# Local-attention transformer block, two calls per kernel: where the layer norm's root is computed, and where a unit's closing work stands among the attention steps

## The chip, the cores and the metric

The kernel runs on one core of a Trainium2 chip, as a single launch. The metric is device time in microseconds (us), taken over several runs, of which the median counts. In the profile the engines are called PE (TensorE, matmul and transpose), PEld (TensorE loading its stationary operand), DVE (VectorE), ACT (ScalarE), POOL (GpSimd) and SP (SyncE, which here only starts DMAs). All data is float32.

## The reference, cut to what matters

The program is four transformer layers in one kernel, each as "half feed-forward, attention, half feed-forward". The change touches only the feed-forward of layer 3, which is itself a small transformer of depth 2 with local attention. It is called twice, with different inputs and the same weights, and the attention of layer 3 (`l3_attn`) stands between the two calls:

```python
x = x + 0.5 * _L3_ffn_ref(_layernorm(x), ...)   # first call
x = x + _L3_attn_ref(_layernorm(x), ...)
x = x + 0.5 * _L3_ffn_ref(_layernorm(x), ...)   # second call, the end of the program
```

`x` has 4 sequences of 512 rows and 128 features. `_L3_ffn_ref` runs this layer twice (8 heads of 64 features, windows of 64 rows, 341 hidden features):

```python
def _layer(x, wqkv, qs, ksc, wo, lg, lb, w1, b1, w2, b2):
    h = shift_token(x)                       # second half of the features comes from the row before
    q, k, v = split(h @ wqkv)                # to 8 heads of 64
    q, k = l2norm(q) * qs, l2norm(k) * ksc   # each head's row divided by its norm
    q, k = rotary_xpos(q, k)
    o = local_attention(q, k, v)             # own window of 64 and the one before; mask, softmax
    x = x + o @ wo
    h = shift_token(x)
    h = (h - mu) / sqrt(var + 1e-05) * lg + lb
    a, g = split(h @ w1 + b1)
    return x + (a * gelu(g)) @ w2 + b2
```

## The kernel before

**Units and steps.** `l3_ffn(w3, tag, first, rb)` is emitted once per call (`first` is true for the first). Its work is 8 *units*: depth 0 for the sequences 0 to 3, then depth 1 for the same sequences. A unit has `TB` = 4 *steps*, one for each 128 rows, so there are 32 steps. The feature-major activations of a sequence lie in `yT`; `x` and `y` are row-major.

**One step** is cut in six parts. The names in brackets are the tiles by which the profile's rows can be followed.

- `project`: the products with the weights of q and k [`p_qk`] and of v [`pv`]; ScalarE squares q and k [`sq`]; VectorE multiplies `p_qk` with the rotary tables in three instructions [`t<-p_qk,w`] and sums the squares to 16 norms a row [`rn`]; `inverse_root` makes the inverse norms of them [scratch `ir`]; GpSimd adds the two rotary parts [`t<-t,t`, L1850] and scales k by its inverse norms [`t<-t,rn`, L1851]; v is copied, and a DMA moves half of it to `vb`.
- `to_features`: eight transposes of q and k [`pt_qk`], copied to `qT` (ScalarE) and `kT` (VectorE).
- `weights`: the products of q and k [`ps`], VectorE's mask addition [`s`], the negative row maximum [`nm`] and its product with q's inverse norms [`nm<-nm,rn`].
- `exponentials`: eight ScalarE instructions, one for each head, with a row sum each [`sm`]; the reciprocal on VectorE, and the product `s<-s,sm` on GpSimd (L1917).
- `turn_weights`: eight transposes [`pt`], copied to `PT`.
- `with_values`: the products with v [`po`], copied to `oT`.

**The closing work of a unit** follows its fourth step: `summed` (product with `wo` [`pz`], added to `yT`), `shifted` (the shifted copy `h`), `centred` (the mean by a product with a constant [`pm`], subtracted: `h<-h,pm`), `squared` (ScalarE, `sq<-h`), `variance` (a product with the same constant [`pvar`], copied to `rs`, and then the root by `inverse_root`), `spread` (VectorE makes diagonal blocks of the root [`dg`]), `normed` (their product [`pb`] scales `h`), three times `hidden` (the two products [`pag`], gelu [`ge`], their product [`hh`]), `close_unit` (product with `w2` [`pz2`], added to `yT`) and, after depth 1, `leave` (transposed back [`pt_z`], added to `x`; in the first call `leave_normed` then starts the next layer norm for `l3_attn`, in the second the rows are stored). `attended` is `summed` and `shifted`, `mean` is `centred` and `squared`. All these take a slice `at` of the unit's 512 rows.

**The order of the work.** A loop over `n` runs from -2 to 37 and emits the six parts in this order, each with a lag, so that several steps are in flight:

```python
for place, (part, lag) in enumerate((
    (project, 0), (to_features, 2), (exponentials, 4), (weights, 3), (turn_weights, 5), (with_values, 6)
)):
    for f, u in later.pop((n, place), ()):
        f(u)
```

A unit's closing work is put among these by a table `parts`: each entry is a function, a number added to `4 * u` to give `n`, and the place ahead of which it is emitted. `squared` has the place `MIDST`, inside `exponentials` after its fifth instruction (`i == 4`). `norm_unit` (the first layer norm of a sequence of depth 0, if the work before the call has not done it) and `open_unit` (the unit's shifted copy `hT`) stand ahead of a unit's first step, at 2 and 1 loop turns.

TensorE and ScalarE execute the products and activations of this layer in the order in which they are emitted. VectorE's and GpSimd's instructions are ordered by the scheduler when the program is built, by what they need; the order of that built program is what the prediction calls the built order.

The last unit (`last` = 7) is not in the table. Its closing work follows the loop as a list `rest`; in the first call it is spread as a *chain* over the start of `l3_attn`, in the second each function is emitted for the first 256 rows and then for the second 256 rows, with `leave` of the unit before behind `attended`.

A chain is a queue of functions with gaps. `tick()`, called after each of the six places (and at such places in `l3_attn`), advances a clock, and a chain's next function is emitted once its gap has passed. `leave_normed(b, chain(b), gap)` puts three functions on one: the row statistics after 1 tick, the scaling (`y`) 1 tick later, and `turn(b)`, four transposes [`pt_y`] copied to `yT`, `gap` ticks later. Statistics, too, end in a root [`ln_r`].

**PSUM.** Bank group "d" has three pairs of banks (`p_qk`, `pt_qk`, `ps`, `pt`, `pag` take turns), group "m" two single ones (`pv`, `po`, `pz`, `pm`, `pvar`, `pb`, `pz2`, `pt_z`, `pt_y`).

**The root.** `inverse_root(sb, dst, src, name, op, c, eng, steps)` has two forms. For up to 4 columns and `steps` false: a `tensor_scalar` on `eng` and a `pow` on GpSimd (L229, L230). Otherwise a bit trick and two rounds of Newton's method, each a row of small instructions on `eng`: 8 on VectorE, 10 on GpSimd (L235 to L245). `rn` (16 columns, L1849) takes the long form on GpSimd; the unit's root in `variance` (4 columns) takes the short form.

In the profile all of VectorE's operations issued by this code appear under L184, TensorE's products under L200 and transposes under L197, ScalarE's under L1789 and, for copies, L1792.

Of the kernel before, what the change touches and what calls it, by code (L numbers as in the profile page):

```python
# [25 lines left out]
ALU = mybir.AluOpType  # L26
# [89 lines left out]
def tile_macaron(ctx, tc, x_in, const_in, vec_in, w0_in, ws_in, ws3_in, w2f_in, w3_in, out):  # L116
# [106 lines left out]
    def inverse_root(sb, dst, src, name, op, c, eng=None, steps=False):  # L223


        n = src.shape[-1]
        if n <= TB and not steps:
            v = sb.tile([P, n], F32, tag=name, name=name, bufs=2)
            (eng or vector).tensor_scalar(v, src, c, None, op)  # L229
            nc.gpsimd.tensor_tensor(dst, v, minus_half[:, :n], ALU.pow)  # L230
            return
        v = sb.tile([P, 3, n], F32, tag=name, name=name, bufs=2)
        eng = eng or vector
        xx, yy, t = (v[:, i, :] for i in range(3))
        eng.tensor_scalar(xx, src, c, None, op)  # L235
        eng.tensor_scalar(yy.bitcast(I32), xx.bitcast(I32), -0.5, float(0x5F1FFFF9), ALU.mult, ALU.add)
        for to, a, b in ((yy, -0.703952253, 1.681913895), (dst, -0.50000016, 1.50000048)):
            eng.tensor_mul(t, yy, yy)
            if eng is vector:
                eng.scalar_tensor_tensor(t, t, a, xx, ALU.mult, ALU.mult)  # L240
                eng.scalar_tensor_tensor(to, t, b, yy, ALU.add, ALU.mult)
            else:
                eng.tensor_mul(t, t, xx)
                eng.tensor_scalar(t, t, a, b, ALU.mult, ALU.add)
                eng.tensor_mul(to, t, yy)  # L245
# [1529 lines left out]
    def l3_ffn(w3, tag, first, rb):  # L1775
        with pool(tag) as sb, banks(tag + "ps", d=3, m=2):
# [48 lines left out]
            def project(step):  # L1825
                u, t = step // TB, step % TB
                l, b = units[u]
                h = u_state[u]["hT"][:, ts(t, P)]
                p = pair("p_qk")
                mm_in_order(p[:, 0:512], h, W(l, "wq"))  # L1830
                mm_in_order(p[:, 512:1024], h, W(l, "wk"))
                pv = bank("m", "pv3")
                mm_in_order(pv, h, W(l, "wv"))

                sq = sb.tile([P, 16, 64], F32, tag="sq", name="sq")
                act(sq.rearrange("p h d -> p (h d)"), p, AF.Square)
                tab = W(l, "tab").rearrange("p (t f i d) -> p t f i d", t=TB, f=2, i=2)[:, t]
                t1 = sb.tile([P, 16, 64], F32, tag="t1", name="t1", bufs=3)
                t2 = sb.tile([P, 16, 64], F32, tag="t2", name="t2")
                by_head = lambda v: v.rearrange("p (i h) d -> p i h d", i=2)  # L1840
                over = lambda v: v[:, :, None, :].to_broadcast([P, 2, 8, v.shape[2]])
                p3 = p.rearrange("p (h d) -> p h d", d=64)
                vector.tensor_mul(by_head(t1), by_head(p3), over(tab[:, 0]))
                for half in range(2):
                    a, z = ts(half, 32), ts(1 - half, 32)
                    vector.tensor_mul(by_head(t2[:, :, a]), by_head(p3[:, :, z]), over(tab[:, 1, :, a]))
                rn = sb.tile([P, 16], F32, tag="rn", name="rn", bufs=6)
                vector.tensor_reduce(rn, sq, AX.X, ALU.add)
                inverse_root(sb, rn, rn, "ir16", ALU.max, 1e-24, nc.gpsimd)  # L1849
                nc.gpsimd.tensor_add(t1, t1, t2)  # L1850
                nc.gpsimd.tensor_mul(t1[:, 8:16, :], t1[:, 8:16, :], bcast(rn[:, 8:16], 64))  # L1851
                v = sb.tile([P, S], F32, tag="v", name="v", bufs=7)
                act_copy(v, pv)

                vb = sb.tile([P, S], F32, tag="vb", name="vb", bufs=7)
                nc.sync.dma_start(vb[64:128], v[0:64])
                if t:
                    nc.sync.dma_start(vb[0:64], s_state[step - 1]["v"][64:128])
                else:
                    light(u).memset(vb[0:64], 0.0)  # L1860
                s_state[step] = {"qk": t1, "rn": rn, "v": v, "vb": vb}
# [42 lines left out]
            def exponentials(step):  # L1904

                midst = later.pop((step + 4, MIDST), ())
                s, nm, rn = (s_state[step][v] for v in ("s", "nm", "rn"))
                sm = sb.tile([P, 8], F32, tag="sm", name="sm", bufs=2)
                for i in range(8):
                    si = s[:, i, :]  # L1910
                    h = 2 * (i % 4) + i // 4
                    act(si, si, AF.Exp, bias=nm[:, i : i + 1], scale=rn[:, h : h + 1], accum_out=sm[:, i : i + 1])
                    if i == 4:
                        for f, u in midst:
                            f(u)
                vector.reciprocal(sm, sm)
                nc.gpsimd.tensor_mul(s, s, bcast(sm, P))  # L1917
# [67 lines left out]
            def variance(u, at=whole):  # L1985

                sq, n = u_state[u].pop(("sq", at.start)), (at.stop - at.start) // P
                pv = bank("m", "pvar")
                for t in range(n):
                    mm_in_order(pv[:, 2 * t : 2 * t + 2], sq[:, ts(t, P)], onesm[:, 0:2])  # L1990
                rs = u_state[u]["rs", at.start] = rb.tile([P, TB], F32, tag="rs", name="rs", bufs=2)
                vector.tensor_copy(rs[:, :n], pv[:, : 2 * n].rearrange("p (t i) -> p t i", i=2)[:, :, 0])
                eng = vector if u == len(units) - 1 else nc.gpsimd
                inverse_root(rb, rs[:, :n], rs[:, :n], f"ir{n}", ALU.add, 1e-5, eng)

            def spread(u, at=whole):

# [41 lines left out]
            def leave(b, at=whole):  # L2039
                pt = bank("m", "pt_z")  # L2040
                t0, n = at.start // P, (at.stop - at.start) // P
                for t in range(n):
                    transpose_in_order(pt[:, ts(t, P)], yT[:, b, ts(t0 + t, P)])
                tiles = slice(b * TB + t0, b * TB + t0 + n)
                xb = x[:, tiles, :].rearrange("p t d -> p (t d)")
                vector.scalar_tensor_tensor(xb, pt[:, : n * P], 0.5, xb, ALU.mult, ALU.add)
                if first:
                    leave_normed(b, chain(b), 3)
                else:
                    nc.sync.dma_start(out[:, tiles, :], x[:, tiles, :])  # L2050

# [16 lines left out]
            if first:  # L2068
                scale_layer(0)

            parts = [
                (summed, 10, 4), (shifted, 10, 5), (centred, 11, 2), (squared, 11, MIDST), (variance, 12, 0), (spread, 12, 2),
                (normed, 13, 0), *((lambda u, c=c: hidden(u, c), 13, 2) for c in range(3)), (close_unit, 14, 0),
                (lambda u: leave(units[u][1]) if units[u][0] else None, 14, 1),
            ]
            later, last = {}, len(units) - 1
            for u in range(len(units)):
                for f, after, place in parts[: -1 if u == last - 1 else None] if u < last else ():
                    if u == last - 1 and f is close_unit:
                        after, place = 13, 5  # L2080
                    later.setdefault((u * TB + after, place), []).append((f, u))
                later.setdefault((u * TB - 2, 0), []).append((norm_unit, u))
                later.setdefault((u * TB - 1, 0), []).append((open_unit, u))
            if first:
                later.setdefault((8, 1), []).append((scale_layer, 1))
            for n in range(-2, n_steps + 6):
                for place, (part, lag) in enumerate((
                    (project, 0), (to_features, 2), (exponentials, 4), (weights, 3), (turn_weights, 5), (with_values, 6)
                )):
                    for f, u in later.pop((n, place), ()):  # L2090
                        f(u)
                    if 0 <= n - lag < n_steps:
                        part(n - lag)
                    tick()
# [3 lines left out]
            if first:  # L2098
                spare = chain(units[last][1])
                for f in rest:  # L2100
                    spare(1, lambda f=f: f(last, whole), f is not spread)
                    if f is variance:
                        spare(1, lambda: leave(units[last - 1][1]))
            else:
                for f in rest:
                    for at in (slice(0, S // 2), slice(S // 2, S)):
                        f(last, at)
                    if f is attended:
                        leave(units[last - 1][1])


    with pool("ws") as wp:
# [241 lines left out]
```

## Time and profile before

| | us |
|---|---|
| median of 3 runs | 2662.89 |
| lowest and highest run | 2661.81, 2663.47 |
| the profiled execution's own time | 2651.55 |
| span of the profile | 2649.8 |

| engine | busy us | share of the span |
|---|---|---|
| PE | 2244.4 | 85% |
| DVE | 1790.2 | 68% |
| ACT | 1307.1 | 49% |
| POOL | 955.0 | 36% |

The profiled execution is one run with the hardware profiler on; its span is the time from its first to its last recorded instruction, and 1.75 us of its own time lie around that. It was shorter than the median by 11.3 us. The mean clock granted to TensorE over the span was 0.912 of full speed.

The first call takes about 1517 to 1945 us of the span, where it overlaps the start of `l3_attn`; the second about 2244 to the end. Each call has a start (the pipeline fills), a middle, in which five units follow each other alike, and an end. TensorE was busy for 66.9 of the 96 us from 1517, 207.7 of the 226 us from 1613 and 74.5 of the 96 us from 1839; in the second call for 77.8 of the 100 us from 2244, 207.7 of the 226 us from 2344 and 63.6 of the last 80 us.

A row of the timeline gives the start, the length, the engine, the line, the operation, out<-in with the shapes, and, in brackets, what TensorE or another engine waited for ahead of it. Rows of equal operations that follow each other closely are merged, with their number behind the "x".

### The profile page before, as it was taken

The numbers are of one execution on the slowest core, as the hardware profiler recorded it, in microseconds if no ns is written. First come the engines' busy times: TensorE is split into PE (matmuls) and PEld (weight loads), VectorE is DVE, ScalarE is ACT, GpSimd is POOL, SyncE is SP. The second block draws the span as 40 slices with busy tenths as digits, with TensorE's granted clock in tenths as the row PEclk, the third lists the DMA queues.
The fourth block names the chain that finished last, engine by engine and source line by source line (L and its number), as shares of the span: only waits on it lengthen the run. The fifth ranks groups of instructions, "written<-read, shape, count | busy, mean of one in ns | idle before, by whom it ended". The sixth has DMA issues, their size and how long they took to land.

```text
span 2649.8 us, 50868 instructions
## 1 busy us (share of the span) xinstructions
PE 2244.4 (85%) x19070; PEld 1277.5 (48%) x19070; DVE 1790.2 (68%) x4787; ACT 1307.1 (49%) x3159; POOL 955.0 (36%) x1535
## 2 busy tenths in 40 slices
PE   6578679989679998988778869998889999798988
PEld 2255234434334444468667735555533333455555
DVE  3745677776666776575555478887557775888874
ACT  3056215444333544344444357776525555677774
POOL 2022113233132322323331388776310000877661
PEclk8689789998779999899878989999879999899998
DMA  3052000000000000237135811010000000111000
GB/s 147 1 168 90 0 1 1 1 1 1 0 1 1 2 1 5 76 115 234 59 109 167 262 34 23 21 23 19 3 1 1 1 1 5 29 23 24 21 21 13
DMA packets 40144, 113.22 MB, mean 43 GB/s; under 512 B 7065, under 2 KB 16537, under 8 KB 39385
## 3 DMA queue, kind: packets, MB, share of 16 engines
q1 hardware_dynamic: 36520, 100.94, 12.0%
q0 software_dynamic: 2944, 6.04, 1.2%
q8 instruction: 151, 2.47, 0.4%
q10 hardware_dynamic: 432, 2.98, 0.3%
q14 instruction: 97, 0.79, 0.1%
HBM read 79.78 MB, written 15.47 MB: 36 GB/s over the span
## 4 chain that ended last, share of the span: by engine, by line
PE 59%; DVE 19%; POOL 9%; ACT 6%; issue 5%; DMA 2%; SPq 0%; POOLq 0%; DVEq 0%; ACTq 0%
PE pk_at L200 10%; PE po_at L200 6%; DVE t L184 4%; PE pa L200 4%; PE pq_at L200 4%; PE pz L200 3%; PE po L200 3%; PE p_qk L200 3%; PE pag L200 3%; PE idle L200 2%; DVE y L184 2%; PE pe L200 2%; PE pg L200 2%; DVE s L184 2%; ACT sq L1789 2%
## 5 line engine op out<-in xcount | busy, mean ns | idle before, releaser
L934 ACT ACTIVATE PT<-pk_at 128x512 f32<-128x512 f32 (+3 forms) x768 | 335.2, 488 | 389.2 <-PE pq_at L200 250.8
L200 PE MATMUL pk_at<-qx,km 32*128 32x512 f32 (+3 forms) x1536 | 396.1, 550 | 5.9 <-ACT PT L934 2.7
L184 DVE CUSTOM_DVE_ANT_0 s<-pq_at,cst 128x384 f32<-128x384 f32 (+3 forms) x512 | 249.4, 487 | 96.6 <-PE pq_at L200 44.4
L200 PE MATMUL pq_at<-km,qT 32*128 32x128 f32 (+3 forms) x1024 | 274.7, 501 | 18.3 <-DVE nm L184 14.4
L1789 ACT ACTIVATE s<-s,nm,rn 128x128 f32<-128x128 f32 x512 | 245.5, 483 | 2.5 <-DVE nm L184 2.3
L937 POOL TENSOR_SCALAR_AFFINE_SELECT PT<-PT 128x256 f32<-128x256 f32 x256 | 104.6, 411 | 374.4 <-ACT PT L934 374.3
L200 PEld LDWEIGHTS pk_at<-qx,km 32*128 32x128 f32 x1536 | 145.6, 189 | 152.3 <-issue 89.6
L200 PE MATMUL po_at<-PT,vh 128*32 128x128 f32 (+3 forms) x2432 | 204.1, 392 | 6.0 <-POOL PT L937 5.9
L184 DVE TENSOR_TENSOR t<-p_qk,w 128x512 f32<-128x512 f32 (+1 forms) x192 | 155.2, 861 | 72.0 <-ACT sq L1789 68.9
L184 DVE TENSOR_REDUCE nm<-pq_at 128x1 f32<-128x512 f32 x256 | 164.7, 684 | 52.5 <-PE pq_at L200 51.0
L1850 POOL TENSOR_TENSOR t<-t,t 128x1024 f32<-128x1024 f32 x64 | 151.1, 2361 | 70.3 <-DVE t L184 62.0
L200 PE MATMUL pq_at<-km,t 32*128 32x512 f32 x512 | 163.7, 657 | 0.1
L200 PE MATMUL p_qk<-w,hT 128*128 128x512 f32 x256 | 134.6, 651 | 15.7 <-DVE t L184 9.9
L1917 POOL TENSOR_TENSOR s<-s,sm 128x1024 f32<-128x1024 f32 x64 | 121.5, 1898 | 67.3 <-DVE sm L184 61.9
L230 POOL TENSOR_TENSOR ln_r<-ir,minus_half 128x4 f32<-128x4 f32 x60 | 62.1, 1035 | 220.3 <-DVE ir L184 219.1
L200 PEld LDWEIGHTS po_at<-PT,vh 128*32 128x32 f32 x2432 | 54.3, 109 | 170.6 <-issue 120.6
L200 PEld LDWEIGHTS pq_at<-km,qT 32*128 32x128 f32 x1024 | 110.1, 190 | 49.0 <-DVE nm L184 28.9
L197 PE MATMUL pt<-ident,s 128*128 128x128 f32 x640 | 90.0, 286 | 44.7 <-POOL s L1917 27.3
L321 ACT COPY yT<-pt_y 128x512 f32<-128x512 f32 x56 | 32.7, 585 | 187.3 <-PE pt_y L197 186.9
L1460 POOL DMA_INDIRECT xg<-yd,come x60 | 57.6, 961 | 172.3 <-PE pt_x L197 71.9
L1789 ACT ACTIVATE sq<-p_qk 128x1024 f32<-128x1024 f32 x64 | 65.5, 1024 | 107.2 <-PE p_qk L200 40.1
L197 PE MATMUL pt_y<-ident,y 128*128 128x128 f32 x224 | 49.8, 345 | 75.4 <-DVE y L184 66.6
(439 smaller groups left out, 5330.3 us busy)
## 6 DMA issues: line engine op xcount, KB each, us to landing
wf<-in_w2f_dram SPq DMA_DIRECT2D x45, 836.0 KB, 5.1
vb<-v SPq DMA_DIRECT2D x112, 128.0 KB, 2.2
w<-in_w2f_dram SPq DMA_DIRECT2D x15, 836.0 KB, 8.6
skew<-qe SPq DMA_DIRECT2D x16, 512.0 KB, 3.0
rel<-skew SPq DMA_DIRECT2D x64, 128.0 KB, 3.5
od<-o SPq DMA_DIRECT2D x60, 64.0 KB, 4.8
w<-in_w_dram SPq DMA_DIRECT2D x1, 3200.0 KB
w<-in_w_dram SPq DMA_DIRECT2D x12, 173.0 KB, 7.6
```

Source lines behind the costliest of these rows:

```text
L184: i = op(*args, **kw)
L197: return nc.tensor.transpose(dst, src, ident[: src.shape[0], : src.shape[0]])
L200: tc.keep_in_program_order(nc.tensor.matmul(dst, lhsT=lhsT, rhs=rhs, start=start, stop=stop))
L230: nc.gpsimd.tensor_tensor(dst, v, minus_half[:, :n], ALU.pow)
L321: by_order(nc.scalar.copy(yT[:, b, :], pt))
L934: by_order(nc.scalar.activation(PT[:, i, q0:], pk[:, q0:], AF.Exp, scale=SC8))
L937: nc.gpsimd.affine_select(d, d, pattern=[[0, 2], [1, P]], base=0, channel_multiplier=-1, compare_op=ALU.is_ge, fill=0.0)
L1460: nc.gpsimd.indirect_dma_start(xT[s], None, yds[k][:, :], bass.IndirectOffsetOnAxis(ap=come[:, i : i + 1], axis=0))
L1789: tc.keep_in_program_order(nc.scalar.activation(*args, **kw))
L1850: nc.gpsimd.tensor_add(t1, t1, t2)
L1917: nc.gpsimd.tensor_mul(s, s, bcast(sm, P))
```

## The change

1. `rn`'s root of the first two steps of a call is computed on VectorE instead of GpSimd.
2. The functions with place `MIDST` (only `squared`) are emitted after the third exponential instead of the fifth.
3. A unit's root in `variance` always takes the long form on VectorE (8 instructions); before, it was a `tensor_scalar` on GpSimd (VectorE for the last unit) and a `pow` on GpSimd.
4. In the first call, `turn(b)` follows the scaling of its chain after 9 ticks instead of 3.
5. In the table, `summed` and `shifted` stand two places earlier, `centred` and `spread` one place earlier.
6. `norm_unit` of units after the first stands one loop turn earlier.
7. In the second call the last unit but one no longer uses the table. Six of its closing functions have places listed for it alone, some beyond the last step's. `summed`, `shifted`, `centred` and `squared` of the last unit's first 256 rows are emitted inside the loop too, ahead of the last step's end. The rest of both units follows the loop as one list, in which unit 6's functions alternate with those of the two halves of unit 7.

```diff
-                inverse_root(sb, rn, rn, "ir16", ALU.max, 1e-24, nc.gpsimd)
+                inverse_root(sb, rn, rn, "ir16", ALU.max, 1e-24, vector if step < 2 else nc.gpsimd)
...
-                    if i == 4:
+                    if i == 2:
                         for f, u in midst:
...
-                eng = vector if u == len(units) - 1 else nc.gpsimd
-                inverse_root(rb, rs[:, :n], rs[:, :n], f"ir{n}", ALU.add, 1e-5, eng)
+                inverse_root(rb, rs[:, :n], rs[:, :n], f"ir{n}", ALU.add, 1e-5, vector, True)
...
-                    leave_normed(b, chain(b), 3)
+                    leave_normed(b, chain(b), 9)
...
-                (summed, 10, 4), (shifted, 10, 5), (centred, 11, 2), (squared, 11, MIDST), (variance, 12, 0), (spread, 12, 2),
+                (summed, 10, 2), (shifted, 10, 3), (centred, 11, 1), (squared, 11, MIDST), (variance, 12, 0), (spread, 12, 1),
                 (normed, 13, 0), *((lambda u, c=c: hidden(u, c), 13, 2) for c in range(3)), (close_unit, 14, 0),
...
-                for f, after, place in parts[: -1 if u == last - 1 else None] if u < last else ():
+                for f, after, place in parts[: -1 if u == last - 1 else None] if u < last - (not first) else ():
...
-                later.setdefault((u * TB - 2, 0), []).append((norm_unit, u))
+                later.setdefault((u * TB - (3 if u else 2), 0), []).append((norm_unit, u))
...
+            one, two = slice(0, S // 2), slice(S // 2, S)
+            if not first:
+                for f, at, place in (
+                    (summed, 2, 0), (shifted, 2, 4), (centred, 3, 5), (squared, 4, 0), (variance, 4, 2), (spread, 5, 2),
+                ):
+                    later.setdefault((n_steps + at, place), []).append((f, last - 1))
+                for f, at, place in ((summed, 4, 1), (shifted, 4, 1), (centred, 4, 5), (squared, 4, 5)):
+                    later.setdefault((n_steps + at, place), []).append((lambda u, f=f: f(u, one), last))
...
-                for f in rest:
-                    for at in (slice(0, S // 2), slice(S // 2, S)):
-                        f(last, at)
-                    if f is attended:
-                        leave(units[last - 1][1])
+                gated = [lambda u, at=whole, c=c: hidden(u, c, at) for c in range(3)]
+                for f, u, at in (
+                    (summed, last, two), (normed, last - 1, whole), (shifted, last, two), (gated[0], last - 1, whole),
+                    (centred, last, two), (variance, last, one), (squared, last, two), (gated[1], last - 1, whole),
+                    (variance, last, two), (gated[2], last - 1, whole), (spread, last, one), (normed, last, one),
+                    (spread, last, two), (normed, last, two), (gated[0], last, one), (close_unit, last - 1, whole),
+                    (gated[0], last, two), (gated[1], last, one), (gated[1], last, two), (gated[2], last, one),
+                    (gated[2], last, two), (close_unit, last, one), (lambda u, at: leave(units[u][1], at), last - 1, whole),
+                    (close_unit, last, two), *((lambda u, at: leave(units[u][1], at), last, at) for at in (one, two)),
+                ):
+                    f(u, at)
```

More of the change, by code (lines that the diff above doesn't have):

```diff
@@ L2104, in l3_ffn @@
             else:
-                for f in rest:
-                    for at in (slice(0, S // 2), slice(S // 2, S)):
-                        f(last, at)
-                    if f is attended:
-                        leave(units[last - 1][1])
+                gated = [lambda u, at=whole, c=c: hidden(u, c, at) for c in range(3)]
[5 more added lines that the diff above has]
+                    (gated[0], last, two), (gated[1], last, one), (gated[1], last, two), (gated[2], last, one),
+                    (gated[2], last, two), (close_unit, last, one), (lambda u, at: leave(units[u][1]), last - 1, whole),
+                    (close_unit, last, two), *((lambda u, at: leave(units[u][1], at), last, at) for at in (one, two)),
+                ):
+                    f(u, at)
     with pool("ws") as wp:
```

## The prediction

> **What bounds the kernel now.** I read the page first (TensorE is busy for 85% of the span), then the stretches of the two calls of the layer, then TensorE's waits in each call, then one step of a unit instruction by instruction. The stretches; columns: start and end, length, busy time (and instructions) of PE, PEld, DVE, ACT, POOL, granted clock, DMA share, GB/s:
>
> ```profile
> 1613.00:1839.00 226.00, 207.68 (x1926) 125.65 (x1916) 188.89 (x256) 169.23 (x442) 163.03 (x290) 1.00 0.10 22
> 2344.00:2570.00 226.00, 207.70 (x1918) 125.78 (x1917) 189.05 (x257) 168.77 (x442) 161.29 (x288) 1.00 0.10 23
> 2570.00:2650.00 80.00, 63.58 (x488) 41.46 (x488) 36.98 (x68) 36.66 (x98) 16.00 (x20) 0.91 0.03 11
> ```
>
> In the middle of each call five units pass in 226 us, 45.1 us each, and TensorE is idle for 18 us of them. That idle time is the most a smoother unit could give. TensorE's waits in the first call (total us, times, longest):
>
> ```profile
> PE pt L197 <- POOL s L1917: 13.4, 6, 4.6
> PE pt_y L197 <- DVE y L184: 10.1, 2, 5.1
> PE pb L200 <- DVE sm L184: 7.8, 5, 1.6
> PE pt L197 <- DVE t L184: 5.9, 6, 1.1
> PE pvar L200 <- ACT sq L1789: 5.1, 6, 1.1
> ```
>
> The last three rows are the middle units: in each, once, pvar waits 0.80, pt 0.95 and pb 1.56 us. Call the four steps after a unit's attention A (n = 4u+10), B, C and D. All three waits lie where B turns to C, and at the end of C. Step C of the third unit (start, length, engine, what):
>
> ```profile
> 1719.79 0.15 DVE L184 COPY rs<-pvar 128x4 f32<-128x4 f32 x1
> ...
> 1720.09 1.04 POOL L1851 TENSOR_TENSOR t<-t,rn 128x512 f32<-128x512 f32 x1
> ...
> 1721.56 1.89 POOL L1917 TENSOR_TENSOR s<-s,sm 128x1024 f32<-128x1024 f32 x1
> 1721.62 2.42 DVE L184 TENSOR_TENSOR t<-p_qk,w 128x1024 f32<-128x1024 f32 x3 [1.68 <-ACT sq L1789]
> ...
> 1723.84 1.04 POOL L230 TENSOR_TENSOR rs<-ir,minus_half 128x4 f32<-128x4 f32 x1
> ...
> 1724.19 1.07 PE L197 MATMUL pt<-ident,s 128*128 128x128 f32 x8 [0.95 <-DVE t L184]
> ...
> 1724.85 2.36 POOL L1850 TENSOR_TENSOR t<-t,t 128x1024 f32<-128x1024 f32 x1
> ...
> 1725.68 2.07 DVE L184 SCALAR_TENSOR_TENSOR dg<-ident,rs 128x512 f32<-128x512 f32 x1
> ...
> 1727.90 1.10 PE L200 MATMUL pb<-dg,onesm 128*128 128x512 f32 x2 [1.56 <-DVE sm L184]
> ```
>
> The root (POOL, 1723.5 to 1724.9) is ready before dg starts: it ends no wait. What is late is dg itself, 2.07 us here and 0.69 us in the three places where POOL is idle: it ends 0.55 us after POOL's t<-t,t. Small operations are held too:
>
> ```profile
> 1685.53 1.04 POOL L1851 TENSOR_TENSOR t<-t,rn 128x512 f32<-128x512 f32 x1
> ```
> ```profile
> 1686.17 0.42 DVE L184 TENSOR_TENSOR nm<-nm,rn 128x8 f32<-128x8 f32 x1
> ```
>
> Eight elements a row, 0.16 us alone, and here it ends 0.02 us after POOL's operation; under s<-s,sm at 2597.28 the same form takes 0.94. Operations with a PSUM input (t, s, hh) keep their time under POOL's. This pair of engines decides the change.
>
> **Ten middle units, A and B.** pz goes ahead of ps, pm ahead of pt_qk: same products, other order, nothing. VectorE's h<-h,pm moves ahead of kT, so it ends 0.6 us sooner (0.68, less overlap). sq follows three exponentials instead of five, and pvar can start at 1717.0 instead of 1717.6. The last exponential ends at 1719.35 instead of 1718.97, which nm (until 1719.67) hides.
>
> **Middle units, C.** Two POOL operations (0.23 + 1.04) go; eight small VectorE ones come. The rows of the layer before, 128x4 on VectorE, give 0.16 us each, started 0.20 apart. In the built order six stand between rs and t, one each after t's first and second third. From 1719.98: the first passes; t<-t,rn holds the second until 1721.15; two more fit before s<-s,sm starts at 1721.56; that holds the fifth until 1723.48; the sixth ends at 1723.7. The three t instructions queue behind: they start at 1723.7, not 1721.62, and with the two operations among them (2 x 0.18) end at 1726.7, not 1724.05. pt waits for them, at 1726.85 instead of 1724.19. POOL's t<-t,t (2.36) starts with t's end and holds dg until 1729.1 + 0.55, so pb starts at 1729.8 instead of 1727.9: **+1.9 us**. The 0.6 gained at pvar is lost in pt's wait. D has no wait now and gets none: h must be done 4.4 us after pb and is done 4.1 after. Ten units: **+19**. Bounds: if nothing holds the roots, t ends at 1724.3, t<-t,t starts there (POOL's root no longer before it), dg ends at 1727.3, pb is 0.45 us sooner: -4.5. If the memset before s<-s,sm holds them too, one operation fewer fits: +2.5 a unit, +25. I take 1.9, from the nm rows, whose form and size are nearest.
>
> [...]
>
> **First call's first steps.** rn's ten POOL operations (3.3 us) go, twice. Step 0: six VectorE operations run until 1528.7, the last two after t<-t,t (1531.21); t<-t,rn starts at 1532.3 instead of 1534.70 and pt_qk's second half 2.5 us sooner. Step 1's eight stand in VectorE's queue behind t<-t,t and ahead of the third step's t, and the layernorm's ln_r now stands behind seven of step 2's POOL operations: pt_y comes at 1547.4 instead of 1545.99. Where p_qk waits for t again (1563.04) I find 0.5 left: **-0.5** (+1.5 to -3).
>
> **Second call's first steps.** The built order puts POOL's second t<-t,t ahead of the first t<-t,rn. So pt_qk's second half waits until 2261.5 instead of 2258.12. yT, now behind sq on ACT, gives some back; p_qk at 2269.97 moves by **+1.0** (-1 to +3).
>
> **The first call's end.** pt_y's 4.97 us wait (1849.66) goes: turn(b) comes six ticks later. What is late next: y still waits for ln_r until 1849.2 and stands ahead of oT and t on VectorE; pm takes oT's bank (1852.2), pvar the next. At pvar 1.8 is left, at pag (1871.78) 0.9, and the 4.64 wait at 1904.24 stays, because sm is still queued behind dg: **-1.0** (0 to -3).
>
> **Second call, sixth unit** (step C at 2571.80): no t here, and the eight stand between s, kT, nm and oT. t<-t,rn and s<-s,sm (2573.13 to 2575.02) hold the second and third, and with them s, which starts at 2575.05 instead of 2572.99; dg, now last, ends at 2580.6 instead of 2577.18, pag starts at 2582.6 instead of 2579.76: **+2.8** (-0.9 to +3.5).
>
> **Second call's last two units.** From the last step's pt (2608.62) to the last pt_z (2646.11) are 37.5 us. Before that point: h now stands behind sm, s<-s,sm starts with sm and holds it 2 us; the last exponentials end at 2605.9, PT and sq follow, pvar, and pt comes when it did. After it: one half's pz (1.86) and pm are gone ahead; the waits for h, rs, dg, yT (0.84, 0.89, 0.38, 0.36) fall under the other unit's products. New: 0.75 for oT, 0.8 for h, 2.2 after unit 6's last pag, where the second half's dg stands on VectorE behind two hh, which wait for ge. Added up product by product I get 32.4. leave(units[6]) moves its 256 KB store (2.3 us to landing, SP's queue) close ahead of the last two of 128 KB: 0 to 2.3, I take 0.1, since issue takes 0.46 and the queue is empty. **-5** (-8 to -1).
>
> **next unit's norm**: norm_unit's chains are finished well before either place and the built order shows nothing moved by it: 0.
>
> Sum: 19 - 0.5 + 1.0 - 1.0 + 2.8 - 5 = **+16.3 us** on the profiled execution's 2651.55. The runs' median is 11.3 above it; the difference carries over: 2662.9 + 16.3 = 2679.2.
>
> **Rivals.** (1) *The chain keeps POOL out.* At 752.4 POOL's PT<-PT took 2.99 us instead of 1.09, because VectorE's two-input operations came without a gap. If the small roots do that, the units give -4.5, the sixth unit -0.9, the starts -3 and -0.5, the end -1.5, the tail -6: -16.4, 2646.5, faster. Against it: those operations overlapped (started 0.20 apart, 0.28 long), while 128x4 ones leave 0.03 to 0.04 between, and POOL's ln_m ran at its normal 0.21 within such a chain at 1148.64. It decides from the unit's price: everything else sums to -2.7, so below +0.3 us a unit the kernel is not slower. Chance 0.30. (2) *Only part is held*: where units settle into another phase, s<-s,sm may start only after the sixth operation, about +0.3 a unit: 2663, no change. For it: pvar is 0.6 sooner. Against: POOL's sequence comes before sm's. Chance 0.08. (3) *The tail gives nothing*, because gelu's table load (1.28 at 2611.65) and hh serialize it: units as forecast, 2684; 0.09. My forecast as worked out: 0.53.
>
> **Numbers.** A measurement here tells 0.2%, 5.3 us, from no change. Faster 0.32 (rival 1 and a large tail), same 0.08, slower 0.60. The range takes in rival 1's 2646.5 and the upper bounds (+25, +3.5, +3, less 1 to 3): 2645 to 2692. The forecast's own range is 2670 to 2690.
>
> **What would show it.** Right: in step C rows of ir on DVE over 0.5 us, t<-p_qk starting some 2 us later after pvar, pt's wait for DVE t about 4 us, units of 47 us, pt_y's wait gone, pt_qk's second wait in call two longer. [...]

## The result and the profile after

The changed kernel took 2691.86 us (median of 4 runs, 2683.23 to 2696.11) against 2662.35 us for the kernel before (4 runs, 2653.46 to 2663.47). The ratio is 1.011, 95% interval 1.009 to 1.013: slower by some 24 to 35 us, where the forecast had +16.3.

The profiled execution took 2696.11 us, 44.6 more than that of before, and not all of this is the change's: the first product of the first call starts at 1534.98 instead of 1519.23, so 15.8 us were lost in the layers ahead of it, which are the same in both kernels. From that product to the end of the span the two traces differ by 1159.43 - 1130.59 = +28.8 us, which fits the runs. All stretches below count from that product, and so leave the varying start out. Call 1's steps 12 to 27 and call 2's hold four middle units each; the fifth unit's step C lies in the stretch behind. The second call's start is counted from the last transpose of `l3_attn` (`pt_ao`), 3.6 to 4.5 us ahead of the call's first product.

| us | start, call 1 | steps 12-27 | end, `l3_attn` | start, call 2 | steps 12-27 | end | all |
|---|---|---|---|---|---|---|---|
| before | 109.1 | 180.3 | 432.4 | 103.6 | 180.3 | 124.8 | 1130.6 |
| after | 107.9 | 194.9 | 434.6 | 103.8 | 194.7 | 123.6 | 1159.4 |
| root_only | 109.2 | 194.6 | 437.6 | 103.0 | 194.5 | 130.5 | 1169.3 |
| root_back | 107.2 | 198.3 | 431.9 | 102.0 | 197.8 | 120.6 | 1157.9 |
| root_back_t | 107.6 | 186.7 | 433.9 | 101.8 | 186.7 | 123.6 | 1140.4 |
| pe_busy | 107.2 | 210.9 | 436.6 | 101.8 | 210.4 | 128.3 | 1195.0 |
| pe_busy2 | 106.6 | 190.1 | 432.9 | 101.8 | 190.1 | 123.2 | 1144.8 |
| root_psum | 107.5 | 175.8 | 431.1 | 101.8 | 175.8 | 125.0 | 1116.8 |
| rest_only | 108.2 | 180.4 | 427.0 | 102.6 | 180.7 | 117.8 | 1116.8 |
| best1 | 107.3 | 175.8 | 430.8 | 102.1 | 175.8 | 115.7 | 1107.5 |
| best1_parts | 108.5 | 175.8 | 431.5 | 104.1 | 175.8 | 114.5 | 1110.1 |
| best2 | 107.5 | 175.8 | 427.6 | 101.8 | 176.1 | 116.1 | 1104.8 |
| psum_old_places | 108.2 | 188.5 | 431.7 | 102.4 | 189.1 | 116.7 | 1136.5 |

A middle unit takes 48.6 to 49.0 us instead of 45.1. The same 226 us of the span as shown of before, which now hold less of the call's work (columns: start and end, length, busy time and instructions of PE, PEld, DVE, ACT, POOL, granted clock, DMA share, GB/s):

```profile
1613.00:1839.00 226.00, 202.41 (x1847) 125.41 (x1846) 204.96 (x276) 160.23 (x429) 150.98 (x274) 0.95 0.10 21
```

VectorE is busy for 16 us more, with only 20 instructions more in the stretch. And the granted clock is 0.95 where it was 1.00. TensorE's waits in the first call:

```profile
PE pt L197 <- DVE t L184: 24.3, 7, 4.3
PE pt_y L197 <- DVE y L184: 8.9, 2, 7.8
...
PE pm L200 <- DVE nm L184: 4.9, 1, 4.9
...
PE pag L200 <- DVE t L184: 4.3, 5, 1.2
...
PE pvar L200 <- ACT sq L1789: 1.5, 6, 0.4
```

pvar's wait shrank as forecast (0.80 to 0.20 in each unit), and the middle units' waits of pb are gone. In their place pt waits 4.3 us for VectorE's t, and pag, in step D, up to 1.2 us where it waited 0.3. Step C of the third unit, instruction by instruction:

```profile
1742.37 0.15 DVE L184 COPY rs<-pvar 128x4 f32<-128x4 f32 x1
...
1742.56 0.17 DVE L184 TENSOR_SCALAR ir<-rs 128x4 f32<-128x4 f32 x1
1742.69 1.04 POOL L1851 TENSOR_TENSOR t<-t,rn 128x512 f32<-128x512 f32 x1
...
1742.76 3.31 DVE L184 TENSOR_SCALAR ir<-ir 128x4 int32<-128x4 int32 x1
...
1743.67 0.52 POOL L1860 MEMSET vb<- 64x512 f32 x1
...
1744.16 1.89 POOL L1917 TENSOR_TENSOR s<-s,sm 128x1024 f32<-128x1024 f32 x1
...
1746.78 1.22 DVE L184 TENSOR_TENSOR t<-p_qk,w 128x1024 f32<-128x1024 f32 x1
...
1749.41 2.35 POOL L1850 TENSOR_TENSOR t<-t,t 128x1024 f32<-128x1024 f32 x1 [3.36 <-DVE t L184]
...
1749.48 1.94 PE L197 MATMUL pt<-ident,s 128*128 128x128 f32 x8 [4.26 <-DVE t L184]
1750.38 1.93 DVE L184 SCALAR_TENSOR_TENSOR dg<-ident,rs 128x512 f32<-128x512 f32 x1
...
1753.26 1.70 PE L200 MATMUL pb<-dg,onesm 128*128 128x512 f32 x2
```

One operation of four elements a row takes 3.31 us: it ends at 1746.07, 0.02 us after s<-s,sm. The whole of GpSimd's sequence passes over it. t, which does not need the root, queues behind. And once pt starts, it takes 1.94 us instead of 1.07, and pb 1.70 instead of 1.10.

### The profile page after: what moved, and what is told of

Its sections match the earlier page's. It is cut to its first block, busy times and chain, and to the rows that moved or that the text cites. A ratio compares the mean times of both kernels' runs of the same rounds, so it can differ in the third digit from the quotient of the medians.

```text
span 2694.4 us, 50991 instructions
## 1 busy us (share of the span) xinstructions
PE 2267.3 (84%) x19070; PEld 1294.0 (48%) x19070; DVE 1871.2 (69%) x4952; ACT 1306.7 (48%) x3159; POOL 928.7 (34%) x1464
## 4 chain that ended last, share of the span: by engine, by line
PE 59%; DVE 25%; POOL 5%; ACT 4%; issue 4%; DMA 2%; another core or an unknown queue 0%; SPq 0%; DVEq 0%; ACTq 0%; POOLq 0%
PE pk_at L200 10%; PE po_at L200 6%; DVE t L184 4%; PE pq_at L200 4%; PE pa L200 4%; PE po L200 3%; PE pz L200 3%; DVE s L184 3%; PE pag L200 3%; PE p_qk L200 2%; PE idle L200 2%; DVE ir L184 2%; PE pe L200 2%; DVE y L184 2%; PE pg L200 2%
## 5 line engine op out<-in xcount | busy, mean ns | idle before, releaser
L1850 POOL TENSOR_TENSOR t<-t,t 128x1024 f32<-128x1024 f32 x64 | 151.3, 2364 | 121.9 <-DVE t L184 116.1
L197 PE MATMUL pt<-ident,s 128*128 128x128 f32 x640 | 97.1, 301 | 71.9 <-DVE t L184 47.4
L1917 POOL TENSOR_TENSOR s<-s,sm 128x1024 f32<-128x1024 f32 x64 | 122.2, 1909 | 89.2 <-DVE sm L184 77.4
L200 PEld LDWEIGHTS po_at<-PT,vh 128*32 128x32 f32 x2432 | 54.4, 109 | 172.8 <-issue 125.0
L200 PEld LDWEIGHTS pq_at<-km,qT 32*128 32x128 f32 x1024 | 110.1, 190 | 49.0 <-DVE nm L184 28.8
L197 PEld LDWEIGHTS pt<-ident,s 128*128 128x128 f32 x640 | 78.3, 153 | 92.6 <-issue 57.0
```

Of the source, the lines that this page charges most:

```text
L197: return nc.tensor.transpose(dst, src, ident[: src.shape[0], : src.shape[0]])
L200: tc.keep_in_program_order(nc.tensor.matmul(dst, lhsT=lhsT, rhs=rhs, start=start, stop=stop))
```

## The experiments

**root_only: the root alone.**

```diff
-                eng = vector if u == len(units) - 1 else nc.gpsimd
-                inverse_root(rb, rs[:, :n], rs[:, :n], f"ir{n}", ALU.add, 1e-5, eng)
+                inverse_root(rb, rs[:, :n], rs[:, :n], f"ir{n}", ALU.add, 1e-5, vector, True)
```

> The kernel before with one edit: a unit's root in eight VectorE steps, every place as before. Theory: of these steps the second is held by GpSimd's t<-t,rn and s<-s,sm until the latter ends, so t<-p_qk starts 4.4 us after rs instead of 1.8, pt waits about 4 us instead of 0.95, and TensorE's clock is granted at about 0.55 behind that wait. Ten middle units of 48.5 us instead of 45.1, +34, and +1 to +4 for the closing work of the last units: 2696 to 2702 against 2662 before. Rival (the earlier places make the units long, not the root): units of 45.1 to 45.5, 2662 to 2667.

(The kernel before took 2650.3 to 2651.2 us in the sessions of all experiments but the last, and 2666.07 in that; so ratios are compared.)

Measured: ratio 1.0136 (1.0118 to 1.0154), 2688.3 us. Units of 48.3 to 49.5 us. The root's place alone makes the units long, and more than the whole loss; the rest of the change gives some of it back.

**root_psum: the same engine, other memory.** The root stays on VectorE. Its scratch moves into pvar's own PSUM bank, and each of its operations reads at least one input from there (two of them are done twice, to have one copy in PSUM and one in SBUF):

```diff
-                vector.tensor_copy(rs[:, :n], pv[:, : 2 * n].rearrange("p (t i) -> p t i", i=2)[:, :, 0])
-                inverse_root(rb, rs[:, :n], rs[:, :n], f"ir{n}", ALU.add, 1e-5, vector, True)
+                got = pv[:, : 2 * n].rearrange("p (t i) -> p t i", i=2)[:, :, 0]
...
+                yp, tp = (pv[:, 64 + i * n : 64 + (i + 1) * n] for i in range(2))
+                vector.tensor_scalar(xs, got, 1e-5, None, ALU.add)
+                for to in (yp, ys):
+                    vector.tensor_scalar(to.bitcast(I32), got.bitcast(I32), -0.5, float(0x5F1FFFF9), ALU.mult, ALU.add)
...
+                    vector.tensor_mul(tp, yp, ys)
+                    vector.scalar_tensor_tensor(tp, tp, a, xs, ALU.mult, ALU.mult)
...
```

> The changed kernel with the root still on VectorE, now ten operations instead of eight and no copy to rs, each with one input in PSUM (pvar's bank holds the scratch). Theory (an operation whose inputs all lie in SBUF is held while GpSimd reads SBUF, one with an input in PSUM is not): each takes 0.15 to 0.2 us also under t<-t,rn and s<-s,sm, t<-p_qk starts 1.3 us after nm, pt waits under 1 us, units of 44.5 to 45.5 us, 2650 to 2660. Rival (the length of the chain of small operations, or their waits for each other): t<-p_qk starts 3 us or more after nm, units of 48 us or more, 2690 or more.

Measured: ratio 0.9955 (0.9939 to 0.9971), 2636.8 us; units of 43.94 us, under those of the kernel before. VectorE in step C of the third unit; GpSimd's t<-t,rn runs from 1711.72 to 1712.76 and s<-s,sm from 1713.19 to 1715.08:

```profile
1711.49 0.16 DVE L184 TENSOR_SCALAR pvar<-pvar 128x4 int32<-128x4 int32 x1
1711.69 0.16 DVE L184 TENSOR_SCALAR iry<-pvar 128x4 int32<-128x4 int32 x1
1711.88 0.17 DVE L184 TENSOR_TENSOR pvar<-pvar,iry 128x4 f32<-128x4 f32 x1
1712.09 0.17 DVE L184 SCALAR_TENSOR_TENSOR pvar<-pvar,irx 128x4 f32<-128x4 f32 x1
1712.29 0.17 DVE L184 SCALAR_TENSOR_TENSOR pvar<-pvar,iry 128x4 f32<-128x4 f32 x1
1712.81 1.23 DVE L184 TENSOR_TENSOR t<-p_qk,w 128x1024 f32<-128x1024 f32 x1 [0.35 <-ACT sq L1789]
```

The bit trick that took 3.31 us takes 0.16, under the same GpSimd work. More operations on the same engine with the same waits for each other made the unit no longer; what they read decides. (One that writes SBUF but has an input in PSUM, iry<-pvar,iry at 1713.95, took 0.15 us under s<-s,sm.) The chain's length and the engine's load fall as causes.

**root_back: the root on GpSimd again.** The root_only edit, reversed, in the changed kernel.

> The changed kernel with one edit: the unit's root goes back to a tensor_scalar and a pow on GpSimd. Theory: units of 44.5 to 45.1 us, rows of ir on VectorE gone from step C, all other parts of the change keep what they showed in the changed kernel's trace (first call's start -1.2, its end -1.0, second call's start +0.2, its end -5): 2652 to 2656, 36 us under the changed kernel. Rival (places): units stay at 48 us, 2688 or more.

Measured: ratio 1.0108 (1.009 to 1.0127), 2678.94 us. A miss: the units became longer still, 49 to 50 us, with no root on VectorE. Its waits in the middle of call 1, and the row that explains them:

```profile
PE pt L197 <- DVE t L184: 27.2, 5, 5.5
```
```profile
1732.50 0.69 DVE L184 SCALAR_TENSOR_TENSOR dg<-ident,rs 128x512 f32<-128x512 f32 x1 [4.99 <-POOL rs L230]
```

With `squared` and `spread` emitted earlier, the scheduler put dg ahead of the three t on VectorE. There dg waits 5 us for GpSimd's root, with t behind it, and pt behind t.

**root_back_t** is root_back with dg pinned behind t:

```diff
-                    vector.tensor_mul(by_head(t2[:, :, a]), by_head(p3[:, :, z]), over(tab[:, 1, :, a]))
+                    i = vector.tensor_mul(by_head(t2[:, :, a]), by_head(p3[:, :, z]), over(tab[:, 1, :, a]))
+                    tc.keep_in_program_order(i)
...
-                vector.scalar_tensor_tensor(
+                i = vector.scalar_tensor_tensor(
                     dg[:, : n * P].rearrange("p (t n) -> p t n", n=P), rows(ident, n), float(D), bcast(rs[:, :n], P),
...
+                tc.keep_in_program_order(i)
```

> root_back with VectorE's dg pinned behind the three instructions t of step C, where the kernel before has it; root_back had it ahead of them, waiting 5 us for GpSimd's root. Theory (that order alone made root_back's units 49 to 50 us; the earlier places and squares themselves gain what pvar gains): units of 44.5 us, ten times 0.6 under the kernel before, and the other stretches as in root_back: 13 to 20 us under the kernel before. Rival (the earlier places cost something else in the middle units): units of 45.1 us or more.

Measured: ratio 1.0038 (1.0026 to 1.0051); units of 46.65 us. Of root_back's 4 to 5 us a unit, some 3 were that order. Part of the rest is dg again:

```profile
1728.25 2.35 POOL L1851 TENSOR_TENSOR t<-t,t 128x1024 f32<-128x1024 f32 x1
...
1728.31 2.84 DVE L184 SCALAR_TENSOR_TENSOR dg<-ident,rs 128x512 f32<-128x512 f32 x1 [0.21 <-POOL rs L230]
```

dg came 0.06 us after GpSimd's t<-t,t and was held for the whole of it, now ahead of kT, the next s and nm on VectorE. In step D nm<-nm,rn took 1.69 us instead of 0.42, and in six of the eight units of steps 12 to 27 pag waited 1.85 us for the t behind it instead of 0.26. So on this kernel the earlier places lost with the root on GpSimd, in both orders tried.

**pe_busy2: what the wait does to the clock.** Three products of 512 columns, whose result is overwritten, are put on TensorE ahead of pt in step C of each middle unit.

```diff
+                if step % TB == TB - 1 and TB < step < n_steps - 2 * TB:
+                    po = s_state[step - 1]["po"] = bank("m", "po3")
+                    for _ in range(3):
+                        mm_in_order(po, onesm, cst[:, :S])
```

> The changed kernel with three products of 512 columns ahead of step C's transposes pt in each middle unit, this time written to the bank that the next products with v overwrite, so that no bank is held longer. Theory (the granted clock of 0.55 behind the wait of 4.26 us is the other part of a unit's price): pt 1.07 us instead of 1.94, pb 1.1 instead of 1.70, units of 47.0 to 47.3 us instead of 48.6, 13 to 16 us under the changed kernel. Rival (the clock behind pt costs nothing, since pb waits for dg anyway): pt at 1.07 and units of 48.4 us or more.

Measured: ratio 1.0065 (1.0041 to 1.0088), units of 47.53 us instead of 48.6, a little above what was expected, though TensorE does 2.84 us more in each. The clock in the changed kernel, during the wait and behind it (columns: start and end, length, PE's busy time, granted clock, DMA share, GB/s):

```profile
1745.30:1749.50 4.20, 0.02 (x1) 0.78 0.14 31
1749.50:1753.00 3.50, 3.50 (x38) 0.50 0.00 0
1753.00:1755.00 2.00, 2.00 (x11) 0.64 0.30 66
```

The same place in pe_busy2, whose granted clock over the middle units is 1.00:

```profile
1721.75 2.84 PE L200 MATMUL po<-cst,onesm 128*128 128x512 f32 x6
1726.07 1.06 PE L197 MATMUL pt<-ident,s 128*128 128x128 f32 x8 [1.48 <-DVE t L184]
1729.07 1.10 PE L200 MATMUL pb<-dg,onesm 128*128 128x512 f32 x2 [0.85 <-DVE dg L184]
```

From pvar to pb: 10.31 us before, 13.69 after, 12.89 here. Less the 0.6 us by which pvar came sooner, pb is 2.0 us late with the clock kept up and 2.8 without, and pb itself loses another 0.6.

The edit changed one thing more: in step D VectorE's order is another, nm<-nm,rn stands ahead of h, and it took 0.34 us instead of 1.68. So the 1.1 us between the units are not the price of the clock alone.

A first form, **pe_busy**, differs in one line: `bank("m", "po3")` is kept for `step` instead of `step - 1`.

> The changed kernel with three products of 512 columns (3.06 us, their result is overwritten) put on TensorE ahead of step C's transposes pt of each middle unit, inside their wait of 4.26 us. Theory (TensorE's granted clock falls to 0.55 behind a wait that long, and this is the part of the unit's price that the forecast lacked): the clock behind pt stays at 1.00, pt takes 1.07 us instead of 1.94, pb 1.1 instead of 1.70, units of 47.0 to 47.3 us instead of 48.6, 13 to 16 us under the changed kernel. Rival (the slower products come from VectorE and GpSimd at work on the same memory, or from nothing that the wait causes): pt at 1.94 as in the changed kernel, units of 48.6 us or longer.

Measured: ratio 1.0254 (1.0236 to 1.0273). pt was at 1.06 us here too, but the bank was held one step too long; pb waited 4.41 us for it, and units took 52 to 53 us. The edit was wrong for its purpose, and says nothing of the price of the wait.

**rest_only: the change without the root and without the middle units' places.** Its diff is the change's, less parts 2, 3 and 5.

> The kernel before with the parts of the change that touch neither the unit's root nor the places of the middle units: rn's first roots on VectorE, turn(b) later, the norm's earlier place, the second call's last two units. Theory: middle units of 45.09 us as before, and the four other stretches -1.5, -1, -2 and -5 to -10: 10 to 14 us under the kernel before. By the forecast's terms (-0.5, -1.0, +1.0, -5): 5 to 6 us under it.

Measured: ratio 0.9953 (0.9935 to 0.997), 2638.11 us; -13.8 us between the traces, the middle untouched. What is left gains more than twice what the forecast's terms gave it.

**best1: each part where it pays.** PSUM root for the units 0 to 4, the root of before for 5 to 7, all else as in the changed kernel (`if u < 5:` around root_psum's code).

> The changed kernel with two kinds of root: ten VectorE operations with inputs in PSUM for the units 0 to 4, whose step C has GpSimd's s<-s,sm and t<-t,rn beside it, and the root of before (GpSimd, VectorE for the last unit) for the units 5 to 7. Theory: middle units of 43.9 us as in root_psum; the first call's end and the second's last 120 us as in root_back, 4 and 10 us under root_psum: ratio to the kernel before 0.989 to 0.992. Rival (the two gains do not add, since a late root on GpSimd delays dg in the sixth unit as VectorE's did): 0.994 to 0.996.

Measured: ratio 0.9918 (0.9894 to 0.9942), 2626.44 us; -23.1 us between the traces. The gains nearly add: 1.15 in each of ten units and rest_only's 13.8 would be 25.3.

**best1_parts** takes two parts out of it: `nc.gpsimd` for rn's first roots, and 3 ticks ahead of `turn(b)`.

> best1 without two parts of the change: rn's roots of the first two steps back on GpSimd, and turn(b) 3 ticks behind the scaling instead of 9. If these parts are worth what the traces suggest (about 1.5 us in each call's start, 1 us at the first call's end), 4 us above best1. As the forecast had them (0.5 gained in the first start, 1.0 lost in the second, 1.0 gained at the end): 0.5 above best1.

Measured: ratio 0.9922 (0.9897 to 0.9948), not to be told from best1 by time. By the traces its starts are 1.2 and 2.0 us longer, the first end 0.6, the last 1.2 us shorter, 2.7 in all: between the two expectations, and closer to the first.

**best2: the earlier places for the middle units alone.**

```diff
+                    if u >= 5:
+                        after, place = {summed: (10, 4), shifted: (10, 5), centred: (11, 2), spread: (12, 2)}.get(f, (after, place))
```

> best1 with the earlier places of summed, shifted, centred and spread for the units 0 to 4 alone, those of before for 5 and 6. Theory: in the first call's end, rest_only, with the places of before and turn(b) at 9 ticks, was 4 us shorter than best1, so these 4 us come back; the middle units stay at 43.9 us and the second call's last 120 us within 2 us of best1: 2 to 5 us under best1. Rival (the 4 us came from the phase in which rest_only reached that stretch, not from the places): within 1 us of best1.

Measured: ratio 0.9915 (0.9899 to 0.993), 2628.61 us. The first call's end is 3.3 us shorter than best1's, as the theory had it, and the middle the same; 2.6 us between the traces is less than the runs can tell.

**psum_old_places** leaves the PSUM root in and takes the earlier places out altogether.

> best1 with the places of before (and squared behind the fifth exponential), so that only the root in PSUM, the first steps' roots, the later turn(b) and the second call's end differ from the kernel before. In the built order dg then stands behind the mask addition s, 1.2 us later than in best1, and t<-t,t has ended by then. Theory (the earlier places are what lets best1 gain in the middle units): units of 44.8 to 45.6 us instead of 43.9, first call's end 4 us shorter than best1's as in rest_only, together 3 to 13 us above best1. Rival (the root in PSUM alone makes the gain): units of 43.9 to 44.2 us, 3 to 5 us under best1.

Measured: ratio 1.003 (1.0018 to 1.0043). Outside both expectations: units of 45.9 to 47.9 us. The scheduler put dg behind the mask addition s, and pb waits for it, 2.25 us a unit:

```profile
PE pb L200 <- DVE dg L184: 11.2, 5, 2.3
```

So neither the PSUM root nor the earlier places gain in the middle units alone; together they give -1.15 us a unit. Of the eight units in the two stretches, two kept a granted clock of 1.00 and took 45.93 us; the other six, with the same waits of pt and pb, fell to 0.96 on the mean and took 47.36 to 47.91.

## Why the prediction was right or wrong, by its steps

**The mechanism** was right: a small VectorE operation of the root with its input in SBUF was held under GpSimd's t<-t,rn and s<-s,sm, 3.31 us; root_psum shows it by changing what the operations read (and doing ten instead of eight), 0.16. It is no rule for every operation that reads SBUF alone, as the theory of root_psum had it: in the kernel before, rn<-sq started at 1570.28, under s<-s,sm (1569.47 to 1571.37), and took the 1.21 us that it takes everywhere (1.20 to 1.22). Rival 1, that the chain keeps GpSimd out, and rival 2, that only part is held, did not happen.

**A middle unit, +1.9.** It cost 3.5 to 4.0 us, 3.6 on the mean, some 36 us over ten units instead of 19. Inside the step one detail differs. No operation passed between GpSimd's three: the second one was held until s<-s,sm had ended, where I let two more through before that; the forecast had named this case as its bound of +2.5 a unit. t started 4.4 us after rs, not 3.9, but ended 7.0 us after it, near what was worked out (6.9): the two small operations among its parts lengthened it by 0.13 us, not by 2 x 0.18, and the forecast's own sum, 1723.7 + 2.42 + 0.36, gives 1726.5 and not 1726.7. dg's end followed that of t<-t,t as worked out (1751.76, and 1752.31 for dg), which made it 2.0 us late; +1.9 was the forecast.

**Two sentences failed: that pb follows dg, and that D "has no wait now and gets none".** The first left out TensorE's clock. Behind the wait of 4.26 us it was granted at 0.50 for about 5 us (0.55 on the mean from 1749.5 to 1755.0), so in the third unit pt and the products with v ended so late that pb came 0.95 us after dg's end, where it was 0.15 before, and pb took 0.6 longer: 2.0 + 0.8 + 0.6 = 3.4 by which pb ended late. The forecast itself said that pt's wait would grow to about 4 us, and the trace of before had the row that prices such a wait: the pt at 1904.24, behind the 4.64 us wait that the page of waits names, took 1.97 us, and the clock there was

```profile
1904.20:1908.00 3.80, 3.76 (x40) 0.50 0.00 0
```

Such a wait has two prices, its length and what follows. In the changed kernel's third unit the clock stood at 0.50 from about 1747.6, 2.4 us into the wait, to about 1754.4 (worked out from the means 0.78, 0.50 and 0.64 shown with pe_busy2); around the wait of 4.64 us in the kernel before, from about 1901.4 to 1908.2 (worked out from the means 0.69 of 1901 to 1902, 0.50 of 1902 to 1908 and 0.90 of 1908 to 1909): 6.8 us both times. Not every wait was followed by this: of root_only's ten waits of 3.24 to 3.26 us, five were followed by a pt of 1.94 and five by one of 1.06 (three of these by a pb of 2.04), and of the changed kernel's ten of 4.2 all were followed by a longer pt (1.18 to 1.94). In psum_old_places pb took 1.38 us or more behind six of ten waits of 2.25 us, so a shorter wait was enough there. What decides between equal waits was not shown.

The second sentence left out the same hold that the forecast had worked out for C. Its own row of nm<-nm,rn, 0.42 us, was one of step D. In all eight units of steps 12 to 27 this operation now started after s<-s,sm and ended with it, t queued behind it, and pag waited for t. The third unit:

```profile
1756.17 1.90 POOL L1917 TENSOR_TENSOR s<-s,sm 128x1024 f32<-128x1024 f32 x1
```
```profile
1756.41 1.68 DVE L184 TENSOR_TENSOR nm<-nm,rn 128x8 f32<-128x8 f32 x1
```

The two prices don't add, since a late pb only uses up time for which pag would wait. In the first unit of that stretch pb ended 0.75 us sooner than in the third, pag waited 1.2 us instead of 0.44, and the unit took the same 48.6 us. Each was also seen without the other. In root_only's second unit the clock stayed at 1.00, and it still took 48.29 us, 3.2 more than before: 2.3 more at pt (3.25) and 0.95 more at pag (1.21), nothing more at pb. In psum_old_places, where pag waited at most 0.53, a fall of the clock made otherwise like units 1.4 to 2.0 longer. pe_busy2, with neither, took 47.53. How the changed kernel's 3.6 split between the two was not tested by a run of its own.

The time, 2691.86, lies past the forecast's own range of 2670 to 2690 and only 0.14 under its outer bound of 2692. That it stayed under is luck: the bound came from a longer hold in C, not from the clock or from D.

**First call's first steps, -0.5**: -1.2. **Second call's first steps, +1.0**: +0.2. pt_qk's second wait did grow (3.5 to 6.4 us, as forecast); more of it was given back than I saw. The nine other kernels with the same code there took 101.8 to 102.6, and the three with the code of before 103.0 to 104.1, so the part rather gains (2.0 us between best1_parts and best1, which differ there in this alone); why the changed kernel's trace shows 103.8 stays open.

**The first call's end, -1.0**: 432.4 to 434.6 is +2.2, with the fifth unit's 3.5 in it, so -1.3. As worked out, pt_y's wait went and VectorE's queue behind y came in its place, but at another point. In best1:

```profile
1837.17 1.04 POOL L230 TENSOR_TENSOR ln_r<-ir,minus_half 128x4 f32<-128x4 f32 x1
1838.25 1.12 DVE L184 TENSOR_SCALAR y<-x,ln_mv,ln_r 128x128 f32<-128x128 f32 x4 [4.00 <-POOL ln_r L230]
...
1841.24 1.19 PE L200 MATMUL pm<-h,onesm 128*128 128x512 f32 x1 [4.92 <-DVE nm L184]
```

y waits 4 us for GpSimd's ln_r, and pm, which the earlier places put ahead of pt_qk and ps, waits behind y. rest_only, with pm where it was, gained 5.4 here, and best2 3.3 over best1. That the earlier pm would stand in front of other products when VectorE is late was not in the forecast, which called its new order "nothing".

**The sixth unit of the second call, +2.8**: pb came at 19.68 us after the last step's p_qk instead of 16.38, +3.3.

**The second call's last two units, -5**: from that pb to the end of the last transposes 60.2 us instead of 68.8, -8.6, past the bound of -8. From the last pt to the last transposes it was 30.3 us against 32.4 worked out; and before that point, where I counted nothing, 1.4 were gained.

The sum: 36 instead of 19 for the units, and -7 instead of -2.7 for all else.

## What to carry to other kernels

Before moving a chain of small VectorE operations, ask what GpSimd runs at that moment and in which memory the chain's inputs lie: one operation of four elements took 3.31 us under t<-t,rn and s<-s,sm, and 0.16 with an input in PSUM. When a forecast makes a TensorE wait longer, look in the trace for a wait of that length and read the rows behind it, since products took nearly twice as long behind the one of 4.26 us (pt 1.94 us instead of 1.07), and look again at every operation that a shift in time may now put under GpSimd's (nm<-nm,rn 1.68 us instead of 0.42). Where a scheduler orders an engine, moving an emission by one place can put a waiting operation in front of the work that matters; the built order has to be read for every combination, and a part that loses alone may gain with another.

## What the runs showed that was not expected

- A VectorE operation was passed by a whole row of GpSimd operations: the 3.31 us run across t<-t,rn, a memset and s<-s,sm, which follow each other without a gap (1742.69 to 1746.05). The held one has a single input, which lies in SBUF; with its input in PSUM it was not held (0.16 us in root_psum), and rn<-sq, also with a single input in SBUF, kept its 1.21 us under s<-s,sm.
- Best measured: best1 and best2, 0.9918 and 0.9915 of the kernel before. How much of VectorE's 4 us wait for ln_r at the first call's end could be had by another place for that root was not tried.
